# Local attention in a decoder kernel: heads of a pair on two halves of the array's rows, grouped scores and values, and VectorE in program order

## The chip, the core and the metric

The kernel runs on one core of a Trainium2 chip. A core has five engines that each work through a queue of their own: TensorE (PE in the profile; its weight loads have a row of their own, PEld), VectorE (DVE), ScalarE (ACT), GpSimd (POOL) and SyncE (SP), which here issues nearly all DMAs. TensorE writes its results to PSUM, a small memory of eight banks of 512 floats on each of 128 partitions; VectorE and ScalarE take them from there to SBUF. The metric is the device time of one execution in microseconds.

## The reference, cut to what matters

Three stages follow one another on 8 sequences of 256 tokens with 128 features. A state-space block and a cross-attention come first; the change touches the third stage, a stack of six layers:

```
for i in range(DEPTH):                     # 6
    x = attn_layer(shift_tokens(x), ...) + x
    x = ffn_layer(shift_tokens(x), ...) + x

def attn_layer(x, Wqkv, qs, ksc, Wo):      # 16 heads of 64 features
    q, k, v = jnp.split(x @ Wqkv, 3, -1)
    q, k = l2norm(q) * qs, l2norm(k) * ksc
    q, k = rotary(q), rotary(k)
    return local_attention(q, k, v) @ Wo

def local_attention(q, k, v):              # windows of 32 queries
    # each window sees its own 32 keys and the 32 before them
    sim = einsum('bhwie,bhwje->bhwij', bq, bk2) * 8
    attn = softmax(where(mask, -max, sim), -1)
    return einsum('bhwij,bhwje->bhwie', attn, bv2)
```

All of it is in 32-bit floats. For one sequence and layer there are 8 windows and 16 heads, so 128 small products of 32 queries by 64 keys over 64 features, and as many of 32 queries by 64 features over 64 keys.

## The kernel before

The third stage is a software pipeline over `n`, which counts pairs of layer and sequence: 6 x 8 = 48 iterations. `run(n)` (L982) walks through a list `slots` (L949), which is written by hand: four quarters, each with one of the four attention tiles of a sequence. A tile `t` is a half `wh` of the sequence (four windows) and a half `g` of the heads (four pairs of two heads). An entry such as `(scores, 0, 2)` calls that function for iteration `n + 0`.

The steps of one tile, in the order of its data:

- `query_key` (L664): two products of 128x512 on TensorE (L656) give queries or keys of 128 tokens; VectorE multiplies them by two tables out of PSUM (L673, L674), GpSimd adds the two parts of the rotation (L677, two instructions), ScalarE squares (L679).
- `squares` (L686), `root` and `normalise` (L705, GpSimd) divide by the norm; `turn` (L712) transposes eight blocks on TensorE, and ScalarE copies them to `qT` (L719) or to the keys `kz` (L725).
- `scores`: 16 products (L760). The rows of the array hold the 128 features of a pair of heads, and the keys `kz` of the two heads stand in two columns blocks with zeros in the other head's rows, so that one product of 128 rows and 128 columns gives both heads' scores. Four windows' heads use four strips of 32 columns of the array at once (`tile_position=(0, i * W)`). VectorE adds the mask (L768) and takes the maximum (L773), GpSimd subtracts it (L774).
- `weigh`: ScalarE's exponential (L94). `add_weights`: VectorE's sum (L786) and reciprocal (L787), and GpSimd's multiplication by it (L788).
- `turn_weights`: four transposes on TensorE (L795) and ScalarE's copy (L799).
- `attend`: again 16 products of 128 rows and 128 columns (L807), with the values `vz` of two heads in blocks among zeros, which `place` has spread by DMA (L745); VectorE transposes the result in blocks of 32 (L817).
- `project_out`: eight products (L826) and VectorE's addition to the stream (L831).

A feed-forward generator runs once for two sequences and is advanced by the entries `("ff",)` and `("late",)`: nine steps over two iterations, with its products at L872, L877, L893 and L921.

A 32-bit product is two pairs of instructions on TensorE, each a weight load and a matmul, so the counts of L760 and L807 in the profile are twice the number of products. Transposes are one pair each.

The order of instructions on an engine: TensorE's is that of the program (`tc.manual_schedule(engines={PE})`, L1134), so the list `slots` is its queue. The other engines' queues are ordered by a planner at build time, which simulates the program and gives an engine, among the instructions that are ready, the one that the program has first. On the chip each queue is then worked through as it stands. In PSUM, tiles come from a pool with three tags: `big` (two of two banks), `s` (two of one bank) and `o` (two of one bank), eight banks in all.

Of the kernel before, what the change touches and what calls it, by code (L numbers as in the profile page):

```python
# [9 lines left out]
FP = mybir.dt.float32  # L10
# [39 lines left out]
def decoder_kernel(ctx: ExitStack, tc: tile.TileContext, a: dict, out: bass.AP):  # L50
# [656 lines left out]
    def turn(n, c, tb):  # L707

        t = got[n][c, tb]
        t_ps = ps_big("qkT_ps")  # L710
        for hb in range(NHB):
            T.transpose(  # L712
                t_ps[:, hb * P : (hb + 1) * P],
                t[:, 2 * hb : 2 * hb + 2, :].rearrange("p h d -> p (h d)"), ident,
            )
# [12 lines left out]
    def spread(v, wh, g):  # L728


        vz = fixed3["vzs"].pop(0)
        fixed3["vzs"].append(vz)
        for j in range(4):
            w = 4 * wh + j
            for e in range(2):

                at = max(0, (w - 1) * W)
                end = (w + 1) * W
                while at < end:
# [5 lines left out]
                    nc.sync.dma_start(  # L745
                        out=vz[k : k + n, j, :, e, :], in_=src[:, 4 * g : 4 * g + 4, e, :]
                    )
                    at += n
        return vz

    def scores(n, t):


        wh, g = tiles3[t]
        qT, kz = got[n]["qT", wh], fixed3["kzs"][0]
        s_ps = ps_s("s3_ps")
        for j in range(4):
            k0 = (4 * wh + j) * W
            for i in range(4):
                T.matmul(  # L760
                    s_ps[i * W : (i + 1) * W, j * P : (j + 1) * P],
                    lhsT=qT[:, 4 * g + i, j * W : (j + 1) * W],
                    rhs=kz[:, 4 * g + i, :, k0 : k0 + 2 * W], start=True, stop=True,
                    tile_position=(0, i * W),
                )
        shape = [P, 4, 2, 2 * W]
        pw = pools3["b"].tile(shape, FP, name="pw", bufs=4)
        V.tensor_tensor(  # L768
            pw, s_ps.rearrange("p (w e k) -> p w e k", w=4, e=2),
            fixed3["mask"][:, 4 * wh : 4 * wh + 4, :].unsqueeze(2).to_broadcast(shape), ALU.add,  # L770
        )
        mx = pools3["b"].tile([P, 2, 4, 2], FP, name="mx", bufs=4)
        V.tensor_reduce(mx[:, 0], pw, AX.X, ALU.max)  # L773
        G.tensor_tensor(pw, pw, mx[:, 0].unsqueeze(3).to_broadcast(shape), ALU.subtract)  # L774
        got[n]["pw", t] = pw, mx

    def place(n, t):
        got[n]["vz", t] = spread([got[n].get(("v", tb)) for tb in range(2)], *tiles3[t])
# [11 lines left out]
    def turn_weights(n, t):  # L790

        pw, mx = got[n]["pw", t]
        t_ps = ps_o("pT_ps")
        for j in range(4):
            T.transpose(  # L795
                t_ps[:, j * P : (j + 1) * P], pw[:, j].rearrange("p e k -> p (e k)"), ident
            )
        pT = pools3["b"].tile([P, 4, P], FP, name="pT")
        turned.append(A.copy(pT.rearrange("p j q -> p (j q)"), t_ps))  # L799
        got[n]["pT", t] = pT  # L800

    def attend(n, t):
        pT, vz = got[n]["pT", t], got[n]["vz", t]
        o_ps = ps_o("o3_ps")
        for j in range(4):
            for i in range(4):
                T.matmul(  # L807
                    o_ps[i * W : (i + 1) * W, j * P : (j + 1) * P],
                    lhsT=pT[:, j, i * W : (i + 1) * W],
                    rhs=vz[:, j, i].rearrange("p e d -> p (e d)"), start=True, stop=True,  # L810
                    tile_position=(0, i * W),
                )

        wh, g = tiles3[t]
        if g == 0:
            got[n]["oT", wh] = pools3["b"].tile([P, NHB, P], FP, name="oT3")
        V.transpose(  # L817
            got[n]["oT", wh][:, 4 * g : 4 * g + 4, :].rearrange("p k (w q) -> p w k q", w=4),
            o_ps.rearrange("p (w k q) -> p w k q", w=4, k=4),
        )  # L820

    def project_out(n, wh):
        d, b = seq[n]
        y_ps = ps_s("y3_ps")
        for hb in range(NHB):
            T.matmul(  # L826
                y_ps[:, :P], lhsT=wts[d][0][:, hb, :], rhs=got[n]["oT", wh][:, hb, :],
                start=(hb == 0), stop=(hb == NHB - 1),
            )
# [95 lines left out]
    def finish(p, b=None):  # L925
# [22 lines left out]
    q, k = 0, 1  # L948
    slots = [  # L949

        (weigh, 0, 1), (place, 0, 1), (value, 1, 0),
        (attend, -1, 3), (scores, 0, 2), (squares, 1, k, 0), (add_weights, 0, 0),
        ("end", 0), (turn, 1, q, 0), ("end", 1), ("ff",),
        (turn_weights, 0, 0), (root, 1, k, 0), ("late",), (query_key, 1, k, 1),
        (normalise, 1, k, 0),

        ("end", 1), (weigh, 0, 2), (place, 0, 2), (project_out, -1, 1),
        (attend, 0, 0), (scores, 0, 3), (squares, 1, k, 1), (add_weights, 0, 1),
        (turn, 1, k, 0), ("end", 0), ("ff",),
        (turn_weights, 0, 1), (query_key, 2, q, 0), (root, 1, k, 1), (normalise, 1, k, 1),  # L960
        (shift, 3),

        (weigh, 0, 3), (place, 0, 3), (value, 1, 1),
        (attend, 0, 1), (scores, 1, 0), (squares, 2, q, 0), (add_weights, 0, 2),
        (turn, 1, q, 1), ("end", 0), ("end", 1), ("ff",),
        (turn_weights, 0, 2), (query_key, 2, q, 1), (root, 2, q, 0), (normalise, 2, q, 0),

        (weigh, 1, 0), (place, 1, 0), (project_out, 0, 0),
        (attend, 0, 2), (scores, 1, 1), (squares, 2, q, 1), (add_weights, 0, 3),
        (turn, 1, k, 1), ("end", 0), ("end", 1), ("ff",),  # L970
        (turn_weights, 0, 3), (query_key, 2, k, 0), (root, 2, q, 1), (normalise, 2, q, 1),
    ]

# [11 lines left out]
    def run(n):  # L985
        nonlocal ff
        for f, *args in slots:
# [7 lines left out]
                    next(end)  # L995
            elif 0 <= n + k < len(seq) and (f, n + k, *args) not in done:
                f(n + k, *args)
                if f is project_out and k < 0:
# [36 lines left out]
    with tc.tile_pool(name="s2", bufs=2, reuse_waits="tile") as sp:  # L1035
# [26 lines left out]
        def values(v, oT, b, hb, w, ws):  # L1062


            o_ps = ps_o("o2_ps")
            for kb in range(2):
                for e in range(2):
                    c = (2 * hb + e) * HD
# [12 lines left out]
            with_table(A.activation, den, den, AF.Exp, scale=-1.0)  # L1081
            V.tensor_tensor(oT[:, hb, b * S : (b + 1) * S], o_ps[:, :S], den, ALU.mult)

        load_table()
        todo = [(b, hb) for b in range(2) for hb in range(NHB)]
        nxt = first
# [32 lines left out]
    with ExitStack() as st:  # L1119
# [3 lines left out]
        nc.sync.dma_start(out=fixed3["mask"], in_=a["c_mask"])  # L1123


        fixed3["kzs"] = [cp.tile([P, NHB, 2, W + S], FP, name=f"kz{i}") for i in range(1)]
        fixed3["vzs"] = [cp.tile([P, 4, 4, 2, HD], FP, name=f"vz{i}") for i in range(3)]
        for t in fixed3["kzs"] + fixed3["vzs"]:
            G.memset(t, 0.0)
        x3.extend(new_x(p) for p in range(NPAIR))  # L1130

        with tc.manual_schedule(engines={mybir.EngineType.PE}):
            shift(1)
            for n in range(-1, len(seq)):  # L1134
                run(n)
            attend(len(seq) - 1, 3)
            for _ in ff:
                pass
            next(end)
# [96 lines left out]
```

## Time and profile before

| | |
|---|---|
| median of 3 runs | 2316.2 us (2311.98 to 2318.99) |
| the profiled execution | 2310.31 us |
| its span, first to last instruction | 2308.5 us |
| granted TensorE clock, mean | 0.976 |
| busy: PE, DVE, ACT, POOL | 2149.5, 1784.3, 1489.8, 1645.3 us |
| third stage alone | from about 690 us to the end |

A row of the profile names the engine, the line of the kernel, the operation, the tile written and the tiles read, the shape, and a count. In the groups, busy time in us and the mean of one in ns follow; behind a bar stands the engine's idle time just before and whose work ended it. In the timeline the first number is the start in us, the second the time from the first start to the last end of a run of like instructions. The end of a matmul is modelled, with its latency in it: what counts for TensorE is from one start to the next.

### The profile page before, as it was taken

Reading aid. Unit: us, or ns where it says so; the run is one execution under the profiler, and the core shown is the slowest. Engines: PE = TensorE matmul, PEld = TensorE weight load, DVE = VectorE, ACT = ScalarE, POOL = GpSimd, SP = SyncE. Lnnn points to the kernel's source line nnn. Section 1 sums busy time; section 2 is a strip of 40 time slices with the busy share of each in tenths; the row PEclk is TensorE's granted clock in tenths of the full one; section 3 lists DMA queues with packets and bytes.
Section 4 is the critical chain, followed back from the end, with each engine's and each line's share of the span. In section 5 each row is a group of like instructions: output and inputs, shape, how many; then the busy total and the mean of one; then the engine's idle time right before and its main releaser. Section 6 shows DMA issues by size and latency. Waiting matters only on the chain.

```text
span 2308.5 us, 52803 instructions
## 1 busy us (share of the span) xinstructions
PE 2149.5 (93%) x20194; PEld 1337.3 (58%) x20194; DVE 1784.3 (77%) x2558; ACT 1489.8 (65%) x2505; POOL 1645.3 (71%) x1437
## 2 busy tenths in 40 slices
PE   7776888999999999999999999999999999999986
PEld 3232333444446666666666666666666666666664
DVE  5798786354558888888888888888888888888873
ACT  4544554455556776776777676777776777777664
POOL 3889795232478878777787777787877777777760
PEclk7988998999999999999999999999999999999999
DMA  4344341000213334333343334343344334333331
GB/s 121 98 113 99 89 110 33 3 3 1 86 26 56 66 61 89 68 72 59 70 80 71 69 63 88 67 73 63 67 81 72 71 62 77 60 64 62 55 67 32
DMA packets 438228, 153.84 MB, mean 67 GB/s; under 512 B 401886, under 2 KB 418140, under 8 KB 437852
## 3 DMA queue, kind: packets, MB, share of 16 engines
q1 hardware_dynamic: 437500, 150.10, 33.1%
q8 instruction: 162, 2.65, 0.5%
q14 instruction: 86, 0.70, 0.1%
q10 hardware_dynamic: 480, 0.38, 0.1%
HBM read 54.68 MB, written 1.31 MB: 24 GB/s over the span
## 4 chain that ended last, share of the span: by engine, by line
PE 31%; ACT 21%; DVE 20%; POOL 9%; issue 6%; DMA 1%; SPq 0%; POOLq 0%; ACTq 0%; DVEq 0%
DVE rb L674 5%; DVE qk L673 5%; PE qk_ps L656 4%; ACT sq L679 4%; ACT kz L725 3%; POOL pw L774 3%; PE f_ps L893 3%; POOL qk L677 3%; ACT pw L94 3%; DVE ss L686 2%; PE qkT_ps L712 2%; PE o_ps L807 2%; PE y_ps L826 2%; PE s_ps L1050 2%; DVE mx L786 2%
## 5 line engine op out<-in xcount | busy, mean ns | idle before, releaser
L677 POOL TENSOR_TENSOR qk<-qk,rb 128x512 f32<-128x512 f32 x384 | 484.5, 1282 | 108.9 <-DVE rb L674 88.8
L705 POOL TENSOR_TENSOR qk<-qk,rn 128x1024 f32<-128x1024 f32 x192 | 366.3, 1908 | 134.5 <-ACT rn L94 107.5
L656 PE MATMUL qk_ps<-wqkv,xs 128*128 128x512 f32 x768 | 364.4, 597 | 2.0 <-ACT sq L679 2.0
L679 ACT ACTIVATE sq<-qk_ps 128x1024 f32<-128x1024 f32 x192 | 196.7, 1025 | 178.1 <-DVE rb L674 174.7
L673 DVE TENSOR_TENSOR qk<-qk_ps,tab 128x1024 f32<-128x1024 f32 x192 | 233.2, 1215 | 80.8 <-PE qk_ps L656 79.9
L774 POOL TENSOR_TENSOR pw<-pw,mx 128x512 f32<-128x512 f32 x192 | 200.2, 1043 | 91.6 <-DVE mx L773 86.2
L686 DVE TENSOR_REDUCE ss<-sq 128x16 f32<-128x1024 f32 x192 | 232.4, 1211 | 39.5 <-ACT sq L679 36.8
L674 DVE TENSOR_TENSOR rb<-qk_ps,tab 128x1024 f32<-128x1024 f32 x192 | 233.0, 1213 | 0.0
L712 PE MATMUL qkT_ps<-ident,qk 128*128 128x128 f32 x1536 | 209.5, 279 | 15.0 <-ACT v L699 9.8
L94 ACT ACTIVATE pw<-pw 128x512 f32<-128x512 f32 x192 | 120.5, 628 | 154.9 <-POOL pw L774 154.7
L725 ACT COPY kz<-qkT_ps 64x1024 f32<-64x1024 f32 x192 | 193.2, 1006 | 35.3 <-PE qkT_ps L712 33.6
L807 PE MATMUL o_ps<-vz,pT 128*32 128x128 f32 x6144 | 207.5, 276 | 8.2 <-ACT pT L799 8.2
L788 POOL TENSOR_TENSOR pw<-pw,mx 128x512 f32<-128x512 f32 x192 | 200.3, 1044 | 19.0 <-DVE mx L787 17.3
L826 PEld LDWEIGHTS y_ps<-oT,wo 128*128 128x128 f32 x1536 | 186.3, 192 | 44.7 <-issue 37.3
L786 DVE TENSOR_REDUCE mx<-pw 128x8 f32<-128x512 f32 x192 | 130.4, 679 | 105.4 <-ACT pw L94 104.8
L807 PEld LDWEIGHTS o_ps<-vz,pT 128*32 128x32 f32 x6144 | 156.0, 109 | 91.8 <-ACT rn L94 35.6
L1059 POOL TENSOR_TENSOR ws<-w 128x512 f32<-128x512 f32 x64 | 81.4, 1272 | 175.6 <-ACT w L94 162.8
L760 PE MATMUL s_ps<-kz,qT 128*32 128x128 f32 x6144 | 203.0, 273 | 0.0
L656 PE MATMUL v_ps<-wqkv,xs 128*128 128x512 f32 x384 | 186.5, 608 | 16.6 <-ACT kz L725 16.6
L712 PEld LDWEIGHTS qkT_ps<-ident,qk 128*128 128x128 f32 x1536 | 165.2, 141 | 55.2 <-issue 43.6
L500 POOL TENSOR_TENSOR mc<-m,rows 128x512 f32<-128x512 f32 x128 | 164.5, 1288 | 40.5 <-PE d_ps L413 18.7
L826 PE MATMUL y_ps<-oT,wo 128*128 128x128 f32 x1536 | 187.2, 275 | 0.1
(187 smaller groups left out, 4163.6 us busy)
## 6 DMA issues: line engine op xcount, KB each, us to landing
vz<-v SPq DMA_DIRECT2D x1152, 64.0 KB, 2.2
rows<-bc_dram SPq DMA_DIRECT2D x126, 256.0 KB, 3.9
vz<-v SPq DMA_DIRECT2D x576, 32.0 KB, 2.3
wqkv<-in_L_ffn_Wqkv SPq DMA_DIRECT2D x18, 512.0 KB, 4.0
wo<-in_L_ffn_Wo SPq DMA_DIRECT2D x48, 64.0 KB, 2.2
w<-in_L_ffn_W SPq DMA_DIRECT2D x6, 341.0 KB, 3.5
t_in<-in_x SPq DMA_DIRECT2D x4, 256.0 KB, 4.7
wkv<-in_L_xattn_Wkv SPq DMA_DIRECT2D x1, 1024.0 KB, 7.8
```

What stands on the lines that cost most here:

```text
L656: T.matmul(pr[:, i * 512 : (i + 1) * 512], lhsT=got[n]["xs"][:, tb * P : (tb + 1) * P], rhs=thirds[seq[n][0], c][:, i * 512 : (i + 1) * 51 ...
L673: V.tensor_tensor(t, p3, cs, ALU.mult)
L674: V.tensor_tensor(rb, p3, sn, ALU.mult)
L677: G.tensor_tensor(t[:, :, o], t[:, :, o], rb[:, :, f], ALU.add)
L679: A.activation(sq, p3, AF.Square)
L686: V.tensor_reduce(got[n]["ss"][:, 2 * c + tb, :], got[n]["sq"], AX.X, ALU.add)
L705: G.tensor_tensor(t, t, r, ALU.mult)
L712: T.transpose(t_ps[:, hb * P : (hb + 1) * P], t[:, 2 * hb : 2 * hb + 2, :].rearrange("p h d -> p (h d)"), ident,)
L725: A.copy(fixed3["kzs"][0][r, :, e, W + tb * P : W + (tb + 1) * P], t3[r])
L774: G.tensor_tensor(pw, pw, mx[:, 0].unsqueeze(3).to_broadcast(shape), ALU.subtract)
L807: T.matmul(o_ps[i * W : (i + 1) * W, j * P : (j + 1) * P], lhsT=pT[:, j, i * W : (i + 1) * W], rhs=vz[:, j, i].rearrange("p e d -> p (e d) ...
L826: T.matmul(y_ps[:, :P], lhsT=wts[d][0][:, hb, :], rhs=got[n]["oT", wh][:, hb, :], start=(hb == 0), stop=(hb == NHB - 1),)
```

## The change

It has these parts, all for the third stage unless said:

- `kz` has no zeros any more: `[P, NHB, W + S]` in place of `[P, NHB, 2, W + S]`, and `turn` writes it in one copy of 128 partitions in place of two of 64.
- `scores` works for a half `wh` of the sequence, thus two tiles in one group. Each product has 64 rows (one head) and 64 columns; the two heads `e` of a pair stand on the halves of the array's rows (`tile_position=(e * HD, i * W)`). There are 64 products in place of 2 x 16. They write to a new PSUM tile of two banks, `ps_two` (one buffer), a bank for each head.
- `masked` (mask and allocation) and `peak` (maximum, and GpSimd's subtraction) are what `scores` did behind its products.
- `attend` likewise: 64 products of 64 rows and 64 columns for two tiles in one group, in the same PSUM tile, and two transposes on VectorE. `vz` is half as large, in six buffers in place of three. `oT` has another layout, which `project_out` reads in four runs of 32.
- `turn_weights` takes its PSUM from tag `s`; the tag `o` is gone here. In the second stage `values` takes the two banks of one `ps_two` in turn.
- `slots` is written anew: scores in the first and third quarter, `attend` in the second and fourth, `project_out` later than before. `add_weights` and `turn_weights` of a tile stay in one quarter, in front of that quarter's `query_key`.
- VectorE's order is that of the program, as TensorE's is.
- The feed-forward's addition of `ff_b` (L880) goes from VectorE to ScalarE.

```
+    def ps_two(name):
+        return banks[-1].tile([P, 2, 512], FP, tag="two", name=name, bufs=1)
...
-            for e in range(2):
-                r = slice(e * HD, (e + 1) * HD)
-                copied.append(
-                    A.copy(fixed3["kzs"][0][r, :, e, W + tb * P : W + (tb + 1) * P], t3[r])
-                )
+            copied.append(A.copy(fixed3["kz"][:, :, W + tb * P : W + (tb + 1) * P], t3))
...
-    def scores(n, t):
...
-            for i in range(4):
-                T.matmul(
-                    s_ps[i * W : (i + 1) * W, j * P : (j + 1) * P],
-                    lhsT=qT[:, 4 * g + i, j * W : (j + 1) * W],
-                    rhs=kz[:, 4 * g + i, :, k0 : k0 + 2 * W], start=True, stop=True,
-                    tile_position=(0, i * W),
-                )
+    def scores(n, wh):
+        qT, kz = got[n]["qT", wh], fixed3["kz"]
+        s_ps = ps_two("s3_ps")
+        for g in range(2):
+            for j in range(4):
+                k0 = (4 * wh + j) * W
+                for i in range(4):
+                    for e in range(2):
+                        r = slice(e * HD, (e + 1) * HD)
+                        c = (4 * g + j) * 2 * W
+                        T.matmul(
+                            s_ps[i * W : (i + 1) * W, e, c : c + 2 * W],
+                            lhsT=qT[r, 4 * g + i, j * W : (j + 1) * W],
+                            rhs=kz[r, 4 * g + i, k0 : k0 + 2 * W], start=True, stop=True,
+                            tile_position=(e * HD, i * W),
+                        )
+        got[n]["s_ps"] = s_ps
...
+    def attend(n, wh):
+        o_ps = ps_two("o3_ps")
+        for g in range(2):
+            pT, vz = got[n]["pT", 2 * wh + g], got[n]["vz", 2 * wh + g]
+            for j in range(4):
+                for i in range(4):
+                    for e in range(2):
+                        r = slice(e * HD, (e + 1) * HD)
+                        c = (4 * g + j) * HD
+                        T.matmul(
+                            o_ps[i * W : (i + 1) * W, e, c : c + HD],
+                            lhsT=pT[r, j, i * W : (i + 1) * W], rhs=vz[r, j, i, :],
+                            start=True, stop=True, tile_position=(e * HD, i * W),
+                        )
+        oT = got[n]["oT", wh] = pools3["b"].tile([P, 2, 2, 4 * HD], FP, name="oT3")
+        for g in range(2):
+            V.transpose(oT[:, g], o_ps[:, :, g * 256 : (g + 1) * 256])
...
-        V.tensor_scalar(xn, xn, col("ff_b", d), None, ALU.add)
+        A.activation(xn, xn, AF.Identity, bias=col("ff_b", d))
...
+        (weigh, 0, 1), (place, 0, 1), (value, 1, 0), (scores, 0, 1), (add_weights, 0, 0),
+        ("end", 0), (masked, 0, 2), (masked, 0, 3), (squares, 1, k, 0), (turn, 1, q, 0),
+        (peak, 0, 2), ("end", 1), ("ff",),
+        (turn_weights, 0, 0), (query_key, 1, k, 1), (root, 1, k, 0), (normalise, 1, k, 0),
+
+        ("end", 1), (weigh, 0, 2), (place, 0, 2), (project_out, -1, 0), (add_weights, 0, 1),
+        (attend, -1, 1), (squares, 1, k, 1), (turn, 1, k, 0),
+        (peak, 0, 3), ("end", 0), ("ff",),
+        (turn_weights, 0, 1), (query_key, 2, q, 0), (root, 1, k, 1), (normalise, 1, k, 1),
+        (shift, 3),
...
-        with tc.manual_schedule(engines={mybir.EngineType.PE}):
+        with tc.manual_schedule(engines={mybir.EngineType.PE, mybir.EngineType.DVE}):
```

The third and fourth quarter are the first and second over again, with other indices; `("late",)` stands in the third in place of the first.

More of the change, by code (lines that the diff above doesn't have):

```diff
@@ L745, in spread @@
                     nc.sync.dma_start(
-                        out=vz[k : k + n, j, :, e, :], in_=src[:, 4 * g : 4 * g + 4, e, :]
+                        out=vz[k : k + n, j, :, :], in_=src[:, 4 * g : 4 * g + 4, e, :]
                     )
@@ L749, in spread, with masked, peak @@
         return vz
-    def scores(n, t):
-        wh, g = tiles3[t]
[L755 to L758, printed above, removed]
-            for i in range(4):
-                T.matmul(
-                    s_ps[i * W : (i + 1) * W, j * P : (j + 1) * P],
-                    lhsT=qT[:, 4 * g + i, j * W : (j + 1) * W],
-                    rhs=kz[:, 4 * g + i, :, k0 : k0 + 2 * W], start=True, stop=True,
-                    tile_position=(0, i * W),
-                )
+    def scores(n, wh):
[15 more added lines that the diff above has]
+        got[n]["s_ps"] = s_ps
+    def masked(n, t):
+        wh, g = tiles3[t]
         shape = [P, 4, 2, 2 * W]
-        pw = pools3["b"].tile(shape, FP, name="pw", bufs=4)
+        pw = pools3["b"].tile(shape, FP, name="pw", bufs=5)
         V.tensor_tensor(
-            pw, s_ps.rearrange("p (w e k) -> p w e k", w=4, e=2),
+            pw,
+            got[n]["s_ps"][:, :, g * 256 : (g + 1) * 256].rearrange("p e (w k) -> p w e k", w=4),
             fixed3["mask"][:, 4 * wh : 4 * wh + 4, :].unsqueeze(2).to_broadcast(shape), ALU.add,
         )
-        mx = pools3["b"].tile([P, 2, 4, 2], FP, name="mx", bufs=4)
+        got[n]["pw", t] = pw, pools3["b"].tile([P, 2, 4, 2], FP, name="mx", bufs=5)
+    def peak(n, t):
+        pw, mx = got[n]["pw", t]
         V.tensor_reduce(mx[:, 0], pw, AX.X, ALU.max)
-        G.tensor_tensor(pw, pw, mx[:, 0].unsqueeze(3).to_broadcast(shape), ALU.subtract)
-        got[n]["pw", t] = pw, mx
+        G.tensor_tensor(pw, pw, mx[:, 0].unsqueeze(3).to_broadcast([P, 4, 2, 2 * W]), ALU.subtract)
     def place(n, t):
@@ L792, in turn_weights @@
         pw, mx = got[n]["pw", t]
-        t_ps = ps_o("pT_ps")
+        t_ps = ps_s("pT_ps")
         for j in range(4):
@@ L797, in turn_weights @@
             )
-        pT = pools3["b"].tile([P, 4, P], FP, name="pT")
+        pT = pools3["b"].tile([P, 4, P], FP, name="pT", bufs=4)
         turned.append(A.copy(pT.rearrange("p j q -> p (j q)"), t_ps))
         got[n]["pT", t] = pT
[L802 to L820, printed above, removed]
+    def attend(n, wh):
[15 more added lines that the diff above has]
+            V.transpose(oT[:, g], o_ps[:, :, g * 256 : (g + 1) * 256])
     def project_out(n, wh):
@@ L826, in project_out @@
             T.matmul(
-                y_ps[:, :P], lhsT=wts[d][0][:, hb, :], rhs=got[n]["oT", wh][:, hb, :],
+                y_ps[:, :P], lhsT=wts[d][0][:, hb, :],
+                rhs=got[n]["oT", wh][:, hb // 4, (hb // 2) % 2, :].rearrange(
+                    "p (w h q) -> p h w q", w=4, h=2
+                )[:, hb % 2],
                 start=(hb == 0), stop=(hb == NHB - 1),
@@ L949, in decoder_kernel @@
     slots = [
[L951 to L959, printed above, removed]
+        (weigh, 0, 1), (place, 0, 1), (value, 1, 0), (scores, 0, 1), (add_weights, 0, 0),
[5 more added lines that the diff above has]
+        (peak, 0, 3), ("end", 0), ("ff",),
         (turn_weights, 0, 1), (query_key, 2, q, 0), (root, 1, k, 1), (normalise, 1, k, 1),
         (shift, 3),
[L963 to L970, printed above, removed]
+        (weigh, 0, 3), (place, 0, 3), (value, 1, 1), (scores, 1, 0), (add_weights, 0, 2),
+        ("end", 0), (masked, 1, 0), (masked, 1, 1), (squares, 2, q, 0), (turn, 1, q, 1),
+        (peak, 1, 0), ("end", 1), ("ff",),
+        (turn_weights, 0, 2), (root, 2, q, 0), ("late",), (query_key, 2, q, 1),
+        (normalise, 2, q, 0),
+        (weigh, 1, 0), (place, 1, 0), (project_out, -1, 1), (add_weights, 0, 3),
+        (attend, 0, 0), (squares, 2, q, 1), (turn, 1, k, 1),
+        (peak, 1, 1), ("end", 0), ("end", 1), ("ff",),
         (turn_weights, 0, 3), (query_key, 2, k, 0), (root, 2, q, 1), (normalise, 2, q, 1),
@@ L997, in run @@
                 f(n + k, *args)
-                if f is project_out and k < 0:
+                if f is project_out and args[0]:
                     d, b = seq[n + k]
@@ L1062, in values @@
         def values(v, oT, b, hb, w, ws):
-            o_ps = ps_o("o2_ps")
+            o_ps = o2_ps[:, hb % 2, :]
             for kb in range(2):
@@ L1082, in values @@
             V.tensor_tensor(oT[:, hb, b * S : (b + 1) * S], o_ps[:, :S], den, ALU.mult)
+        o2_ps = ps_two("o2_ps")
         load_table()
@@ L1123, in decoder_kernel @@
         nc.sync.dma_start(out=fixed3["mask"], in_=a["c_mask"])
-        fixed3["kzs"] = [cp.tile([P, NHB, 2, W + S], FP, name=f"kz{i}") for i in range(1)]
-        fixed3["vzs"] = [cp.tile([P, 4, 4, 2, HD], FP, name=f"vz{i}") for i in range(3)]
-        for t in fixed3["kzs"] + fixed3["vzs"]:
+        fixed3["kz"] = cp.tile([P, NHB, W + S], FP, name="kz")
+        fixed3["vzs"] = [cp.tile([P, 4, 4, HD], FP, name=f"vz{i}") for i in range(6)]
+        for t in [fixed3["kz"]] + fixed3["vzs"]:
             G.memset(t, 0.0)
         x3.extend(new_x(p) for p in range(NPAIR))
-        with tc.manual_schedule(engines={mybir.EngineType.PE}):
+        with tc.manual_schedule(engines={mybir.EngineType.PE, mybir.EngineType.DVE}):
             shift(1)
@@ L1135, in decoder_kernel @@
                 run(n)
-            attend(len(seq) - 1, 3)
+            project_out(len(seq) - 1, 0)
+            attend(len(seq) - 1, 1)
             for _ in ff:
```

## The prediction

> **What bounds the kernel now.** I read the shares by engine first (PE 93%, DVE 77%, POOL 71%), then the timeline of TensorE in the steady part of the third stage, because a share alone doesn't say whether an engine is waited for. One quarter of an iteration:
>
> ```profile
> 1407.09 1.08 PE L807 MATMUL o_ps<-vz,pT 128*32 128x128 f32 x32
> 1407.98 1.06 PE L760 MATMUL s_ps<-kz,qT 128*32 128x128 f32 x32
> 1408.97 1.09 PE L712 MATMUL qkT_ps<-ident,qk 128*128 128x128 f32 x8
> 1409.90 1.46 PE L921 MATMUL f_ps<-fh,w 128*128 128x256 f32 x6
> 1411.20 0.60 PE L795 MATMUL pT_ps<-ident,pw 128*128 128x128 f32 x4
> 1411.64 1.88 PE L656 MATMUL qk_ps<-wqkv,xs 128*128 128x512 f32 x4
> 1413.36 1.88 PE L656 MATMUL v_ps<-wqkv,xs 128*128 128x512 f32 x4
> 1415.17 1.08 PE L807 MATMUL o_ps<-vz,pT 128*32 128x128 f32 x32
> ```
>
> No row waits: TensorE goes from one piece to the next, so its work sets the pace. From start to start: values 0.89, scores 0.99, transposes 0.93, feed-forward 1.30, weights' transposes 0.44, queries 1.72, values' projection 1.81. The quarters repeat every two iterations (eight quarters; start to start of L795: 8.28, 7.71, 9.94, 7.71, 8.75, 8.15, 8.08, 7.50), 66.1 us or 8.27 a quarter, 24 times over.
>
> The one stall of L795 on the weights' multiplication is at the start of the stage, and it shows a path that the steady part keeps slack on. I took these rows from the timeline of all engines:
>
> ```profile
> 702.66 2.74 PE L656 MATMUL qk_ps<-wqkv,xs 128*128 128x512 f32 x4
> ...
> 705.44 1.22 DVE L673 TENSOR_TENSOR qk<-qk_ps,tab 128x1024 f32<-128x1024 f32 x1 [1.91 <-PE qk_ps L656]
> ...
> 706.59 1.21 DVE L674 TENSOR_TENSOR rb<-qk_ps,tab 128x1024 f32<-128x1024 f32 x1
> ...
> 707.72 0.19 DVE L787 RECIPROCAL mx<-mx 128x8 f32<-128x8 f32 x1
> ...
> 708.14 2.51 POOL L677 TENSOR_TENSOR qk<-qk,rb 128x512 f32<-128x512 f32 x2
> ...
> 710.61 2.05 POOL L788 TENSOR_TENSOR pw<-pw,mx 128x512 f32<-128x512 f32 x2
> ...
> 711.71 0.66 PE L795 MATMUL pT_ps<-ident,pw 128*128 128x128 f32 x4 [1.68 <-POOL pw L788]
> ```
>
> The reader is to see that the reciprocal is done at 707.9, but GpSimd's multiplication L788 stands behind the two sums of the rotation (L677) and starts at 710.61, and that L795 waits for it. From the modelled end of the queries (702.66 + 2.74 = 705.40) to L795 it took 6.31. In the steady part L788 ends 3.4 to 11 us ahead of its L795, because the planner has moved the sum L786 and its reciprocal ahead of L673 on VectorE.
>
> **The change, part by part.** *Row halves.* The trace has no matmul of 64 rows by 32 columns. Nearest are these groups:
>
> ```profile
> L807 PE MATMUL o_ps<-vz,pT 128*32 128x128 f32 x6144 | 207.5, 276 | 8.2 <-ACT pT L799 8.2
> ...
> L1050 PE MATMUL s_ps<-qT,kT 64*128 64x256 f32 x512 | 73.8, 402 | 3.3 <-ACT sq L679 2.9 <-DVE w L1056 0.3
> ```
>
> L807 keeps four column strips going: 32 matmuls in eight turns of 0.109 us, in each of which the four start 0.007 apart. L1050 (row halves, two banks) takes 1.07 for eight matmuls of 256 columns, where one after another would need about 8 x 0.215 = 1.72, so halves of the rows do run at once. With eight tiles and 64 columns a turn is about 0.056, and a group of 128 matmuls has 16 turns: 0.90 at best. Against that, issue: the records of TensorE's semaphore instructions, 16 instructions apart, stand 0.125 apart with 0.051 for themselves, so about 4.6 ns an instruction, and 256 instructions take 1.2. The Trainium skill speaks against the change here: "TensorE: Matmul & The Clock Gate", section "Wait — 56ns, not 53.3ns?", says that matmuls never start less than about 25 ns apart however few columns they have. By that rule a group costs 128 x 0.025 = 3.2. The average of L807, 0.109 / 4 = 27 ns, does not refute it; starts 7 ns apart on different strips do, for short runs. I take 1.1, nearer to the trace, and keep 0.9 and 3.2. A quarter has one such group in place of L807 and L760, with one entry and one exit of the tiled mode as before: 1.88 becomes about 1.2, **0.7 less in 192 quarters, 134 us of TensorE's time**. By the page's rule it would be 1.4 more, 270 us.
>
> *Key copies:* 192 of 1006 ns become 96 of about 1012 (the row of the queries' copy): 96 us less on ScalarE, which waits and isn't the bound; nothing, hidden under TensorE. *The bias* L880 leaves VectorE (1831 ns, 24 times) for ScalarE (about 650, by L94 on the same shape): nothing on the path. *DMAs:* the same nine a tile with the same runs; SyncE issues each in about 0.65, 5.9 of 8.3 a quarter, still enough. Six buffers end its waits for L807, of which no reader waits. *One PSUM tile* for scores and values: a quarter lies between a group and the next, and VectorE reads it within about 2 us of its end; nothing unless VectorE is over 4 us late. *The memset* of kz halves, from 3.9: at most 2 us once. *Second stage:* the same two banks in turn; nothing.
>
> *VectorE in program order* is what decides. In `slots`, `add_weights` stands behind the `query_key` of the quarter before, so L786 and L787 now come behind L673 and L674. GpSimd's two sums are ready when L674 ends, the multiplication only 0.9 later, and the sums are first in the program too; the planner will queue sums, multiplication. `turn_weights` of the same tile and then `query_key` stand at the end of that same quarter on TensorE. This closes a loop, once a quarter: queries from start to modelled end 1.88; VectorE starts 0.04 behind; L673 and L674 2.35 (the median in the trace); 0.08; two sums 2.50; L788 1.04; 0.05; L795 0.44, and the next queries. **Sum 8.38.** The one occurrence above gives 6.31 + 0.49 + 1.88 = 8.68. I take 8.45. All waiting of other engines hangs on this loop: behind L795 on TensorE stand the queries, and so VectorE's and ScalarE's next work; what TensorE saves becomes its wait for L788 (own work up to L795: 1.81 + 1.2 + 0.93 and on average 1.2 of feed-forward, 5.1, while the loop lets L795 go at 6.1).
>
> Only the quarter with the three upward products (6 x 0.43 = 2.58) is longer by TensorE: 1.81 + 1.2 + 0.93 + 2.58 + 0.44 + 1.72 = 8.7. Eight quarters: 7 x 8.45 + 8.7 = 67.9, against 66.1: +1.8, 24 times, **+43**. The first six quarters, where TensorE has little to do (6.9 to 7.6 now), become 8.45: +8. GpSimd's table work at five layer borders (eight instructions, 3.3 us, of which 1.5 shows now) falls into the loop: up to +1.8 each, I take +5. Memset -2. Together +54 on the profiled 2310; the median stands 6 above that execution, so the forecast is 2316 + 54 = **2370 us**.
>
> **Rivals.** *GpSimd multiplies before the sums, or between them.* The loop loses 1.25 to 2.5, TensorE bounds again, and 0.7 x 8 = 5.6 is gained 24 times: 2316 - 134 = 2182 us. It decides as soon as the loop falls under 8.27, only 0.2 less than I take. For it: the order is a planner's, which I can't see. Against it: at the start of the stage, and at 1400.75, where a reciprocal had been issued at 1400.31, the sums went first; nothing stands between the two sums anywhere in the trace. *Issue bounds the groups* by the page's 25 ns: TensorE reaches L795 2 us later, the loop no longer matters, 9.6 a quarter: 2316 + 250 = about 2570. It decides from about 17 ns a matmul. *The loop is slack but VectorE's order is not:* its work of 6.9 a quarter plus waits at the head of its queue bounds at about 8: 2265 us. *Nothing happens:* the halves don't run at once; then a group costs 1.8 as before, and the loop still rules: the main case.
>
> **How the numbers follow.** Loop bound 0.68 (its own range 2322 to 2425: loop 8.3 to 8.7); multiplication first 0.20 (2150 to 2240); VectorE 0.04; issue 0.08. A measurement of this kernel tells 0.3%, 7 us, from no change. Slower: 0.63 of the main case and 0.08; same 0.03; faster 0.20 + 0.04 + 0.02 of the main case. Leaving out the lower part of the second case and the issue case, the range is 2180 to 2430.
>
> **What would show it.** Right: L795 waits for POOL L788 in nearly every quarter, about 1 us; TensorE's busy time falls by some 130 us while the span grows; POOL's queue reads sums, multiplication; L807 and L760 take 0.9 to 1.3 a group. Wrong: TensorE without gaps and a quarter of 7.6, or groups over 2 us.

## The result, and the profile after

The changed kernel takes 2406.5 us (median of 4, 2402.7 to 2411.4), the kernel before beside it 2314.1 (2310.4 to 2319.0): a ratio of 1.040, 95% interval 1.038 to 1.041. It is slower by 92 us; I had forecast 54. The page of the kernel after: its engine totals, its instruction queue (packets, MB), its chain by line, and two of its groups (busy us, mean ns of one | idle just before, and what ended it):

```profile
PE 2131.7 (89%) x32482; PEld 1297.4 (54%) x32482; DVE 1742.5 (73%) x2533; ACT 1423.0 (59%) x2438; POOL 1645.6 (69%) x1440
...
q8 instruction: 255, 4.18, 0.8%
...
POOL qk L681 17%; PE qk_ps L660 13%; POOL pw L799 7%; DVE qk L677 7%; DVE rb L678 6%; PE pT_ps L806 5%; PE f_ps L907 2%; PE y_ps L837 2%; PE o_ps L1083 2%; PE pr L241 2%; PE v_ps L660 2%; PE s_ps L1064 2%; PE s_ps L764 2%; PE y_ps L1121 1%; PE o_ps L823 1%
...
L677 DVE TENSOR_TENSOR qk<-qk_ps,tab 128x1024 f32<-128x1024 f32 x192 | 234.9, 1224 | 297.3 <-PE qk_ps L660 297.3
...
L806 PE MATMUL pT_ps<-ident,pw 128*128 128x128 f32 x768 | 127.6, 289 | 137.3 <-POOL pw L799 134.3
```

The line numbers have moved: the queries are L660 (before L656), their two multiplications L677 and L678 (L673, L674), the sums of the rotation L681 (L677), the sum and reciprocal of the weights L797 and L798 (L786, L787), GpSimd's multiplication L799 (L788), the transposes of the weights L806 (L795), scores L764 (L760), values L823 (L807).

The first six entries of the chain are one circle: queries, two multiplications, rotation, multiplication of the weights, transposes. TensorE's transposes L806 stood 134 us behind L799, in 145 of the 192 quarters (0.9 us each), where L795 had hardly stood at all. One turn of the circle, from the timeline of the kernel after:

```profile
1402.30 0.66 PE L806 MATMUL pT_ps<-ident,pw 128*128 128x128 f32 x4
...
1402.79 1.88 PE L660 MATMUL qk_ps<-wqkv,xs 128*128 128x512 f32 x4
...
1404.71 1.23 DVE L677 TENSOR_TENSOR qk<-qk_ps,tab 128x1024 f32<-128x1024 f32 x1 [0.73 <-PE qk_ps L660]
1405.85 1.22 DVE L678 TENSOR_TENSOR rb<-qk_ps,tab 128x1024 f32<-128x1024 f32 x1
1406.39 1.77 PE L823 MATMUL o_ps<-vz,pT 64*32 64x64 f32 x128
...
1407.21 2.51 POOL L681 TENSOR_TENSOR qk<-qk,rb 128x512 f32<-128x512 f32 x2 [1.56 <-PE o_ps L823]
1407.89 0.20 DVE L798 RECIPROCAL mx<-mx 128x8 f32<-128x8 f32 x1
1408.09 1.09 PE L716 MATMUL qkT_ps<-ident,qk 128*128 128x128 f32 x8
...
1409.68 1.04 POOL L799 TENSOR_TENSOR pw<-pw,mx 128x512 f32<-128x512 f32 x1
...
1410.77 0.66 PE L806 MATMUL pT_ps<-ident,pw 128*128 128x128 f32 x4 [0.30 <-POOL pw L799]
```

The reciprocal is done at 1408.09, but GpSimd is in its sums until 1409.7, and only then multiplies. From one L806 (1402.30) to the next (1410.77) is 8.47. (A releaser such as "PE o_ps L823" on L681 is only the last event that the profile saw; the sums needed L678, which ended then.) The group of values takes 1.70 here from its start to the start of the next piece, not 1.2.

Where the 92 us lie can be read from the first and the last of the weights' transposes, in the views of these lines of before and after (shortest, median and longest of a matmul in ns; first and last start):

```profile
L795 PE MATMUL pT_ps<-ident,pw x768: 270/273/421, 693.5 to 2269.3; 128*128 128x128 f32 x192
```

```profile
L806 PE MATMUL pT_ps<-ident,pw x768: 271/273/474, 707.5 to 2346.1; 128*128 128x128 f32 x192
```

| part of the span, us | before | after | more | forecast |
|---|---|---|---|---|
| to the first weights' transposes | 693.5 | 707.5 | +14.0 | -2 |
| from there to the last | 1575.8 | 1638.6 | +62.8 | +56 |
| from the last to the end | 39.2 | 54.8 | +15.6 | 0 |
| span | 2308.5 | 2400.9 | +92.4 | +54 |

So the loop, on which the forecast rested, has about the size it was given. What was missing is mostly in two stretches outside the steady part, 16 us each.

### The profile page after: what moved, and what is told of

Same layout as the page of the kernel before. It is cut to its first block, busy times and chain, and to the rows that moved or that the text cites. A ratio compares the mean times of both kernels' runs of the same rounds, so it can differ in the third digit from the quotient of the medians.

```text
span 2400.9 us, 76914 instructions
## 1 busy us (share of the span) xinstructions
PE 2131.7 (89%) x32482; PEld 1297.4 (54%) x32482; DVE 1742.5 (73%) x2533; ACT 1423.0 (59%) x2438; POOL 1645.6 (69%) x1440
## 3 DMA queue, kind: packets, MB, share of 16 engines
q8 instruction: 255, 4.18, 0.8%
## 4 chain that ended last, share of the span: by engine, by line
PE 39%; POOL 26%; DVE 16%; issue 3%; ACT 3%; DMA 1%; SPq 0%; POOLq 0%; ACTq 0%; DVEq 0%
POOL qk L681 17%; PE qk_ps L660 13%; POOL pw L799 7%; DVE qk L677 7%; DVE rb L678 6%; PE pT_ps L806 5%; PE f_ps L907 2%; PE y_ps L837 2%; PE o_ps L1083 2%; PE pr L241 2%; PE v_ps L660 2%; PE s_ps L1064 2%; PE s_ps L764 2%; PE y_ps L1121 1%; PE o_ps L823 1%
## 5 line engine op out<-in xcount | busy, mean ns | idle before, releaser
L681 POOL TENSOR_TENSOR qk<-qk,rb 128x512 f32<-128x512 f32 x384 | 481.7, 1277 | 182.6 <-DVE rb L678 137.6
L677 DVE TENSOR_TENSOR qk<-qk_ps,tab 128x1024 f32<-128x1024 f32 x192 | 234.9, 1224 | 297.3 <-PE qk_ps L660 297.3
L660 PE MATMUL qk_ps<-wqkv,xs 128*128 128x512 f32 x768 | 369.4, 604 | 2.2 <-ACT kz L726 1.1
L786 POOL TENSOR_TENSOR pw<-pw,mx 128x512 f32<-128x512 f32 x192 | 202.3, 1054 | 91.0 <-DVE mx L785 90.8
L806 PE MATMUL pT_ps<-ident,pw 128*128 128x128 f32 x768 | 127.6, 289 | 137.3 <-POOL pw L799 134.3
L678 DVE TENSOR_TENSOR rb<-qk_ps,tab 128x1024 f32<-128x1024 f32 x192 | 233.2, 1214 | 0.0
L806 PEld LDWEIGHTS pT_ps<-ident,pw 128*128 128x128 f32 x768 | 81.7, 142 | 251.6 <-POOL pw L799 248.5
L799 POOL TENSOR_TENSOR pw<-pw,mx 128x512 f32<-128x512 f32 x192 | 200.8, 1046 | 15.8 <-DVE mx L798 12.7
L810 ACT COPY pT<-pT_ps 128x512 f32<-128x512 f32 x192 | 112.5, 586 | 146.1 <-PE pT_ps L806 143.2
L660 PEld LDWEIGHTS qk_ps<-wqkv,xs 128*128 128x128 f32 x768 | 133.5, 194 | 98.8 <-issue 95.2
L482 PE MATMUL y<-mc,ident 128*128 128x512 f32 x256 | 148.9, 699 | 42.0 <-POOL mc L504 41.8
L660 PE MATMUL v_ps<-wqkv,xs 128*128 128x512 f32 x384 | 180.6, 592 | 0.3 <-ACT sq L683 0.3
L502 DVE TENSOR_TENSOR_SCAN m<-dw,ab 128x256 f32<-128x256 f32 x256 | 159.9, 668 | 26.1 <-POOL mc L504 21.8
L764 PEld LDWEIGHTS s_ps<-kz,qT 64*32 64x32 f32 x12288 | 137.6, 105 | 74.4 <-DVE qk L677 69.0
```

The source lines that it names most:

```text
L660: T.matmul(pr[:, i * 512 : (i + 1) * 512], lhsT=got[n]["xs"][:, tb * P : (tb + 1) * P], rhs=thirds[seq[n][0], c][:, i * 512 : (i + 1) * 51 ...
L677: V.tensor_tensor(t, p3, cs, ALU.mult)
L678: V.tensor_tensor(rb, p3, sn, ALU.mult)
L681: G.tensor_tensor(t[:, :, o], t[:, :, o], rb[:, :, f], ALU.add)
L786: G.tensor_tensor(pw, pw, mx[:, 0].unsqueeze(3).to_broadcast([P, 4, 2, 2 * W]), ALU.subtract)
L799: G.tensor_tensor(pw, pw, mx[:, 1].unsqueeze(3).to_broadcast([P, 4, 2, 2 * W]), ALU.mult)
```

## The experiments

The theory: the order of VectorE and GpSimd closes the loop, and TensorE waits in it. Rivals: TensorE itself is the bound, because 128 small matmuls cost it too much; or VectorE's program order as such is harmful, whatever stands in it.

**e1: the sum of the weights ahead of the queries.** One entry of `slots` is moved in each quarter, from behind the previous quarter's `query_key` to ahead of it:

```diff
-  (scores, 0, 1), (add_weights, 0, 0),
+  (scores, 0, 1),
 ...
-  (turn_weights, 0, 0), (query_key, 1, k, 1), (root, 1, k, 0), ...
+  (turn_weights, 0, 0), (add_weights, 0, 1), (query_key, 1, k, 1), (root, 1, k, 0), ...
```

and so in the other three quarters.

> Changed kernel with one thing moved: add_weights of the next quarter stands ahead of query_key in each quarter, so VectorE sums a tile's weights before it touches the queries, and GpSimd multiplies (L799) before it adds the rotation (L681). Loop theory: the wait of the weights' transposes L806 for L799 (137 us) goes, TensorE sets the pace again with what the smaller groups leave of its work, 66.1 - 8 x 0.25 = 64.1 us in eight quarters against 68.5 now; 24 x 4.4 = 106 us less, and the slow first quarters with them: 2280 to 2305 us. TensorE theory (the groups of 128 small matmuls cost so much that TensorE is the bound by itself): 2395 to 2415. Theory that VectorE's program order as such bounds, whatever stands in it: 2380 to 2415, with the wait of L806 moved to another line.

Measured: 2255.5 us, ratio to before 0.975 (0.974 to 0.977), 151 us less than the changed kernel. The timeline of e1:

```profile
1403.10 0.68 DVE L797 TENSOR_REDUCE mx<-pw 128x8 f32<-128x512 f32 x1
...
1403.81 0.20 DVE L798 RECIPROCAL mx<-mx 128x8 f32<-128x8 f32 x1
...
1404.27 1.23 DVE L677 TENSOR_TENSOR qk<-qk_ps,tab 128x1024 f32<-128x1024 f32 x1 [0.26 <-PE qk_ps L660]
...
1405.73 1.04 POOL L799 TENSOR_TENSOR pw<-pw,mx 128x512 f32<-128x512 f32 x1
...
1406.73 2.50 POOL L681 TENSOR_TENSOR qk<-qk,rb 128x512 f32<-128x512 f32 x2
...
1408.91 0.60 PE L806 MATMUL pT_ps<-ident,pw 128*128 128x128 f32 x4
```

GpSimd now multiplies ahead of the sums, and the product is there 2 us before L806 at 1408.9. L806's waits for L799 in this run come to 2.8 us. Eight quarters (starts of L806: 7.52, 9.90, 7.43, 8.16, 8.01, 7.74, 7.00, 6.84) take 62.6 us against 68.5 after and 66.1 before. I had expected 64.1 from groups of 1.6; about half of the 1.5 us between is waits of TensorE that the kernel before had and this one has not (26.5 us for L656, L712 and L893 between 780 and 2100 us there, 13.5 for L907 here). So both rivals fall: the same groups of matmuls on TensorE, and VectorE in program order as well, are faster than the kernel before.

**e2: VectorE in program order alone**, in the kernel before.

```diff
-  with tc.manual_schedule(engines={mybir.EngineType.PE}):
+  with tc.manual_schedule(engines={mybir.EngineType.PE, mybir.EngineType.DVE}):
```

> Kernel before with one thing of the change: VectorE also in program order; its slots, its groups of 32 matmuls over 128 rows and its planner for GpSimd stay. In these slots the sum of the weights stands behind the mask and maximum of the scores of the same quarter, so the loop is longer than in the changed kernel: queries 1.7, values' projection 1.8 (every second quarter), values 0.9, scores 1.0, mask and maximum 1.2, squares 1.1, sum and reciprocal 0.7, multiplication 1.04, transposes 0.44, so 8.2 to 10.1 a quarter, 9.3 on average against 8.27. Loop theory: 2316 + 192 x 1.0 = about 2510 (2420 to 2620). TensorE theory (order is harmless, the groups cost): 2310 to 2325.

Measured: 2969.4 us, ratio 1.286 (1.279 to 1.292). The direction is the loop's, the size was far off (2420 to 2620 expected). L795 waits in nearly every quarter, from TensorE's waits in e2:

```profile
PE pT_ps L795 <- POOL pw L788: 461.8, 190, 4.5
```

A quarter takes 10.6 where the clock is full, since in these slots mask, maximum and squares all stand between the scores and the sum of the weights on VectorE. My sum had 9.3: it left out the output projection (L826, 1.9 us), which stands in the loop in every quarter that has no values' projection. More than half of the quarters take 11.5 us or more. There TensorE's clock is low: the queries take 2.7 to 3.6 us in each of them (3.47 at 1498.54) and 1.88 in the others, and the run's mean clock is 0.898. The kernel before lives from the planner's order of VectorE.

**e3: row halves, groups and slots alone**, the change with VectorE given back to the planner (the line of e2 reversed).

> Changed kernel with VectorE given back to the planner: row halves, two tiles in one group and the new slots stay. Loop theory: the planner takes the sum of the weights as soon as it is ready, GpSimd multiplies early, L806 hardly waits, TensorE bounds at about 8.0 a quarter: 2275 to 2305. TensorE theory: 2395 to 2415. The second stage keeps its later end (stage three's first weights' transposes near 707 us instead of 693) by either.

Measured: 2336.7 us, ratio 1.010 (1.008 to 1.011). Better than the changed kernel by 70, worse than before by 23, and not the 2275 to 2305 that the loop theory said. The loop is open (4.1 us for L799 in all), but the planner's order gives TensorE other waits, here those of the whole run:

```profile
PE f_ps L907 <- ACT sq L683: 18.2, 43, 0.6
PE pT_ps L806 <- DVE x L845: 17.9, 22, 0.9
...
PE y_ps L837 <- DVE ln_xc L887: 10.7, 21, 0.6
PE y_ps L837 <- DVE x L936: 10.7, 22, 0.6
```

With two smaller ones they come to 61 us between 780 and 2100, or 3 in eight quarters: 66.6 against e1's 62.6. So row halves, groups and new slots together bring nothing under the planner's order, and e1, with program order on VectorE and the sum in its place, is 81 us faster than e3. What each part is worth alone is not shown: no run has the row halves in the old slots. In the three parts of the span, e3 has +18.1, -9.3 and +16.7 against before.

**e4: two PSUM tiles in the second stage.** In the change the values of the second stage are halves of one tile that lives through the whole stage; here they are two tiles taken in turn, in a pool of their own that is closed before the third stage takes the banks.

```diff
-  o_ps = o2_ps[:, hb % 2, :]
+  o_ps = twos[-1].tile([P, 512], FP, tag="o", name="o2_ps")
```

> Changed kernel with the second stage's values in two PSUM tiles of one bank each that are taken in turn, as before the change, instead of two halves of one tile; the third stage's double tile is opened behind it in the same banks. If the halves of one tile are held apart only as a whole (TensorE waits 51 times, 37.8 us, for the division L1096 of the pair just before), these waits go and everything of the third stage starts 12 to 15 us earlier: 2390 to 2396. If the later start of the third stage came from elsewhere (memsets, loads, the planner's order): 2403 to 2410.

Measured: 2389.9 us, 16.6 less than the changed kernel; the first weights' transposes start at 693.9, as before the change (693.5). What had delayed them is in the view of the line L1083 of the kernel after, the idle time ahead of it (us, times; weight loads and matmuls together):

```profile
its engine sat idle before it (us, times) until:
  DVE oT L1096: 37.8, 51
```

The first product of most pairs waited for the division of the pair just before, though that reads the other bank. The program's waits are set by whole tiles, so a writer of one half also waits for the reader of the other. With two tiles these waits are 4.1 us, five times.

**e5 and e9: work put into TensorE's waits at the start.** The first quarters of the third stage last 10.1 us in the changed kernel (starts of L806 from 707.5: 10.1, 10.1, 10.1, 10.2, 10.1, then 8.5). TensorE's timeline there:

```profile
717.57 1.09 PE L806 MATMUL pT_ps<-ident,pw 128*128 128x128 f32 x4 [4.33 <-POOL pw L799]
718.46 3.17 PE L660 MATMUL qk_ps<-wqkv,xs 128*128 128x512 f32 x4
721.47 1.88 PE L660 MATMUL v_ps<-wqkv,xs 128*128 128x512 f32 x4
...
727.72 1.02 PE L806 MATMUL pT_ps<-ident,pw 128*128 128x128 f32 x4 [1.94 <-POOL pw L799]
728.54 3.25 PE L660 MATMUL qk_ps<-wqkv,xs 128*128 128x512 f32 x4
```

and its clock, from the table by stretches of the same kernel (the granted clock is the third number from the right):

```profile
730.00:740.00 10.00, 6.62 (x145) 4.04 (x144) 6.02 (x8) 3.96 (x10) 6.42 (x5) 0.84 0.24 41
...
760.00:770.00 10.00, 8.16 (x161) 5.38 (x160) 7.16 (x9) 6.28 (x12) 7.61 (x7) 1.00 0.38 66
```

The same queries take 1.88 or 3.2: just behind the wait they run at about half speed, and they lie in the loop. The Trainium skill, "TensorE: Matmul & The Clock Gate", Part 1, tells of such a gate that halves the clock after about 3.4 us without work. In this trace gaps of 1.8 and 1.9 us were followed by slow queries too. The test adds products that nobody reads ahead of L806:

```diff
+  w_ps = ps_s("warm_ps")
+  for _ in range(3 if n else 6):       # e5, n < 2; e9: 2, in the first six quarters
+      T.matmul(w_ps, lhsT=ident, rhs=thirds[0, 0][:, :512], start=True, stop=True)
```

> Changed kernel with work added: ahead of the weights' transposes L806 of the first two iterations stand 6 (first) or 3 (second) matmuls 128x128 by 512 columns whose result nobody reads, 36 in all or 15.5 us at 0.43 each, in time in which TensorE waited 1.6 to 4.3 us. Clock theory (the first five quarters take 10.1 us instead of 8.5 because TensorE, having waited, runs the transposes and the queries at half speed, 1.1 instead of 0.66 and 3.1 to 3.5 instead of 1.88): with the matmuls the queries stay at 1.88 and the first five quarters at 8.4 to 8.8; 6 to 9 us less, 2396 to 2401. If the long quarters come from loads or from the planner's order: 2406 to 2420.

Measured for e5: 2410.9 us, ratio 1.042 (1.040 to 1.044). I had counted a product as one matmul; it is two, so the added work filled more than the waits, and the time came out where the rival (loads, the planner's order) had put it. The rows speak for the clock all the same: it was 1.00 throughout, and the queries took 1.88 in every one of these quarters.

> As e5, with less added work: 2 matmuls of 512 columns ahead of L806 in each of the first six quarters only. In e5 one such matmul showed as two rows of 0.43, so e5 added 46 us of TensorE's time (5.3 or 2.7 a quarter), about all that the clock gave back. Here it is 1.77 us a quarter in waits of 1.6 to 4.3. Clock theory: the queries stay near 1.88 in most of these quarters, the first five take 8.5 to 9.0 instead of 10.1, 5 to 8 us less than the changed kernel's 2406.5: 2398 to 2402. If so little work does not hold the clock, or the clock is not what makes these quarters long: 2406 to 2412.

Measured for e9: 2403.0 us, ratio 1.038 (1.037 to 1.040), which overlaps with the change's, and lies between the two ranges expected. The rows are clearer than the time: six quarters of 8.39 to 8.51, and as soon as the added work ends, the slow quarter comes (10.1).

```profile
723.90 0.66 PE L810 MATMUL pT_ps<-ident,pw 128*128 128x128 f32 x4
724.39 1.88 PE L660 MATMUL qk_ps<-wqkv,xs 128*128 128x512 f32 x4
...
757.71 0.75 PE L810 MATMUL pT_ps<-ident,pw 128*128 128x128 f32 x4 [1.94 <-POOL pw L799]
758.25 3.53 PE L660 MATMUL qk_ps<-wqkv,xs 128*128 128x512 f32 x4
```

So the clock is why the first quarters were 10.1 and not 8.45: the first six take 50.7 us here and 59.1 in the changed kernel. Not all of these 8.4 us stay in the sum, since one slow quarter comes later; from the first transposes to the last it is 1634.3 against 1638.6. Where the limit lies is not settled: in e9 gaps of 2.0 and 2.1 us left the clock at 1.00, and one of 1.94 was followed by queries of 3.53.

**e6: what a group of small matmuls costs.** Three more passes over the scores of eight iterations, with 32 columns (L788), with one row half only (L791), and with the halves in the outer loop (L794):

```diff
+  again([(g, j, i, e) for g in R2 for j in R4 for i in R4 for e in R2], 32, half)
+  again([(g, j, i, 0) for g in R2 for j in R4 for i in R4], 64, one_row_half)
+  again([(g, j, i, e) for g in R2 for j in R4 for e in R2 for i in R4], 64, e_outer)
```

> Changed kernel with three more passes over the scores' group in 8 of its 48 iterations, one behind the other ahead of the mask: 128 matmuls with 32 columns instead of 64 (into half of the columns, so those hold the same scores), then the 64 of one row half alone with 64 columns, then 128 with 64 columns and the row half as the outer loop of each turn. If instructions cost a fixed time each (1.55 us for 128 is 12 ns each), the passes take about 1.55, 0.78 and 1.55. If columns set the time (64 columns and eight tiles at once, plus a fixed part), 32 columns take 0.9 to 1.0, the single half 0.9 to 1.5. If the alternation of row halves costs, the third pass is under 1.3. The time of the whole is longer by 8 x 2 x about 3 us and tells nothing more.

The timeline of TensorE in e6:

```profile
1131.11 1.52 PE L764 MATMUL s_ps<-kz,qT 64*32 64x64 f32 x124
1132.40 0.21 PE L788 MATMUL s_ps<-kz,qT 64*32 64x32 f32 x1
...
1132.47 1.62 PE L788 MATMUL s_ps<-kz,qT 64*32 64x32 f32 x116
1135.88 0.23 PE L788 MATMUL s_ps<-kz,qT 64*32 64x32 f32 x4 [1.78 <-issue]
...
1135.97 1.01 PE L791 MATMUL s_ps<-kz,qT 64*32 64x64 f32 x58
1136.76 0.24 PE L794 MATMUL s_ps<-kz,qT 64*32 64x64 f32 x1
...
1136.82 0.77 PE L794 MATMUL s_ps<-kz,qT 64*32 64x64 f32 x54
1139.62 1.32 PE L794 MATMUL s_ps<-kz,qT 64*32 64x64 f32 x71 [2.04 <-issue]
```

64 columns: 1.29 us for 124 matmuls, 10.4 ns each. 32 columns: 1.62 less the last one's own 0.2, for 116, 12.2 ns each. One row half, thus four tiles: 0.79 for 58, 13.6 ns each. The halves in the outer loop: 0.77 less 0.2 for 54, 10.6 ns each ahead of the pause, so their alternation is not what costs. With eight tiles half the columns don't save time, and what is left is a cost of each matmul with its weight load: 10 to 12 ns, so by estimate 5 to 6 an instruction. So it went as the first of the three cases, except for the single row half. That should have taken 0.78 us and takes 0.87 (64 x 13.6), near the lower end of what I gave for columns (0.9 to 1.5): its four tiles start within 0.056 us, which is the turn of 64 columns that the prediction has. So with four tiles columns can still set the time.

The starts of the single records add one thing. In the changed kernel the first 32 matmuls of every group, in all 192, start 8.3 ns apart, close to the 7 of eight tiles in a turn of 0.056. The other 96 start 11.6 (scores) and 12.6 ns (values) apart in the median. A short run keeps the pace that I took for the whole group; a long one does not. Why it slows down is not shown. The pauses of 1.8 and 2.0 us were not expected either; see the end.

**e7 and e8: the multiplication done twice**, in the changed kernel (e7) and in e1 (e8), to see whether the loop has the length that the sum gives it.

```diff
+  twice = pools3["b"].tile([P, 4, 2, 2 * W], FP, name="twice", bufs=1)
+  G.tensor_tensor(twice, pw, mx[:, 1].unsqueeze(3).to_broadcast([P, 4, 2, 2 * W]), ALU.mult)
   G.tensor_tensor(pw, pw, mx[:, 1].unsqueeze(3).to_broadcast([P, 4, 2, 2 * W]), ALU.mult)
```

> Changed kernel with the multiplication L799 of the weights done twice on GpSimd (first into a scratch tile), 192 instructions of 1.04 us more on an engine that is busy 69%. Loop theory: each lies in the loop; seven quarters of 8.46 become 9.50 and the one of 9.30 becomes 9.5: 76.0 instead of 68.5 in eight, 24 x 7.5 = 180 us more and 5 at the start: 2570 to 2610. Theory that TensorE or VectorE's order bounds and GpSimd has slack: 2405 to 2430.

> The same doubled multiplication in the kernel of e1, where the sum of the weights stands ahead of the queries on VectorE. Loop theory: there the product is done a whole quarter ahead of its reader, GpSimd's work of 6.5 + 1.04 = 7.5 us a quarter is still under TensorE's 62.6 / 8 = 7.8: 2255 to 2290. If GpSimd's multiplication sets the time wherever it stands: 2255 + 180 = about 2435.

Measured: e7 2664.4 us, ratio 1.151 (1.149 to 1.153), 258 more than the changed kernel; e8 2290.7, ratio 0.990 (0.989 to 0.992), 35 more than e1. The same 192 instructions, 200 us of GpSimd, cost more than their length in the loop and a sixth of it outside. In e7 the steady quarter is 9.59 against 8.47, a step of 1.12 for one instruction of 1.04; the quarter with the three upward products went from 9.30 to 10.35, not to 9.5 as I had it; and 33 of the 191 quarters took 10.9 to 12, twelve at the start and the others scattered. In each of these the queries take 2.8 to 3.6 us, in all others 1.88. So behind the longer waits the low clock comes into the steady part too (the run's mean is 0.950 against 0.971), which is why e7 is above what I expected.

**e10 and e11: what the findings give together.** e10 has the edits of e1 and e4; e11 has ScalarE in program order too, behind the last iteration.

> The edits of e1 and e4 together: sum of the weights ahead of the queries, and two PSUM tiles for the second stage's values. The two act in different stages, so their gains add: 2255.5 - (2406.5 - 2389.9) = about 2239 (2235 to 2245). If the third stage's start is held by its loads as well, only a part: 2245 to 2255.

> e10, and behind the last iteration ScalarE is issued in program order too, so the three Gelu of one feed-forward stand together: 5 loads of activation tables fewer (1.28 us each) on ScalarE in the last 40 us, in which TensorE waited up to 5 us for it. If ScalarE's tables make the end longer (from the last weights' transposes to the end 56 us against 39.5 before the change): 6 to 12 us less than e10, about 2230. If the end is longer only because more work is left behind the last transposes: within 3 us of e10.

Measured: e10 2235.6 us, ratio 0.967 (0.965 to 0.968); e11 2231.3, ratio 0.965 (0.963 to 0.966). The two edits of e10 add, as expected. e10 beats both kernels, by 79 and 171 us. e11 cannot be told from e10 by the time. Behind the last weights' transposes e10 loads eight activation tables, e11 four (1.28 us each), but the time from there to the end only fell from 55.0 to 52.1. So tables are the smaller part of the longer end. TensorE's own rows there show the two parts: from the last transposes to the end it works 33.7 us in the changed kernel and 23.3 in the one before, and waits 18.0 and 12.9. In e11 the work is still 33.9 and the waits are 15.0. The longest wait there, before and after, is for the normed input of the upward products. In the changed kernel two instructions of the norm's root (L98) and the addition of `ff_b` (L894) stand among five loads of tables on ScalarE; in e11 this wait is gone.

```profile
2282.84 1.56 PE L893 MATMUL f_ps<-fxn,w 128*128 128x256 f32 x6 [1.75 <-DVE fxn L880]
```

```profile
2372.30 2.93 PE L907 MATMUL f_ps<-fxn,w 128*128 128x256 f32 x6 [5.03 <-ACT fxn L894]
```

## Why the prediction was right or wrong

- **The loop, right.** L806 waits for L799, GpSimd's queue reads sums, multiplication, and the loop has 8.41 to 8.49 against the 8.45 taken. e1 removes it by one entry's place, e7 lengthens it by about what one more instruction takes (1.12 for 1.04).
- **"8.7" for the quarter with the upward products, mis-sized:** 9.30. Eight quarters are 68.5, not 67.9. The term held a group at 1.2; in the quarter from 1444.62 to 1453.92 us it takes 1.62, which is 0.42 of the 0.6. The rest is in the upward products (2.73 for 2.58) and the transposes.
- **"A group of 128 matmuls: 1.1", mis-sized:** 1.52 (scores) and 1.61 (values) in the median, from a group's start to the next piece's. I had 4.6 ns an instruction, from records of semaphores; e6 shows 5 to 6, and the fast pace lasts for 32 of the 128 matmuls. With it goes "134 us of TensorE's time": its busy time fell by 18, and by 59 in e1. For the changed kernel's time it mattered little, as the loop hid it; for the rival "GpSimd multiplies first" it is most of the reason why e1, which does just that, gives 2255 and not 2182; start and end are 29 of these 73 us. The page's 25 ns a matmul, which I set against it, does not hold for tiles of the array that differ: 8 to 14 ns.
- **"Second stage: the same two banks in turn; nothing", failed:** +14. The banks are the same, but what waits is decided by the tile, and there was now one. e4 shows it.
- **"First six quarters: +8", mis-sized:** the first six take 59.1 against 46.7, +12.4. Two errors met here. The six quarters of the kernel before are not all "6.9 to 7.6": the first two took 8.3 and 9.9, so the loop alone makes +4 (6 x 8.45 = 50.7). And the clock was not thought of: the waits that the loop brings slow down the very products in it, which is the other 8.4 (e9 has 50.7).
- **The end of the kernel was not in the sum, failed:** +15.6. It is there in e1 and e3 as well (+16.7), so it comes neither from the loop nor from VectorE's order. By TensorE's rows 10.4 of it is work that the new slots leave behind the last transposes: a second output projection, and 2.0 us of upward and 3.1 of downward products ahead of the last one. The other 5.1 is waits, and e11 takes 3 of it away. "The bias: nothing on the path" holds but for this end, where the addition on ScalarE comes some 1.3 us later than it did on VectorE.
- **Layer borders +5 and the steady +43:** the stretch behind the first six quarters has +50.4 for +48, in part by luck. By the medians the steady part is 2.4 longer in eight quarters (68.5 against 66.1) and not 1.8, some 55 us over the 185 quarters. Against that, four layer borders cost no more than before (about 1.0 over the median, 1.5 before), and the last eleven quarters are shorter by 5.
- **Signs:** L806's wait and GpSimd's order came as named. TensorE's busy time fell by 18, not by some 130, and the groups take more than 1.3.

The range held the time, and so did the main case's own, 2322 to 2425. The direction was earned: the loop came as summed. That 2406 still lies in the range is luck in part: start, first quarters and end, 36 of the 38 us that were missing, were not what the range stood for (a loop of 8.3 to 8.7), and they all made the kernel slower.

## What to carry to other kernels

When an engine's order becomes that of the program, follow one result around all engines until it comes back to its start, and sum one turn of that loop: here an entry that stood one call too late cost 151 us, and moved it made the change a gain. A saving on the busiest engine counts only when no such loop is longer than that engine's work, and a wait that such a loop brings can lower TensorE's clock and so lengthen itself. When two buffers are joined into one tile, look whether readers and writers of its halves are still held apart.

## What the runs showed of the hardware

TensorE's small matmuls on eight different tiles of its array start 8.3 ns apart for the first 32 of a group of 128 in the changed kernel, and 11 to 13 ns behind. In e6, right behind such a group, it was 12 ns with 32 columns as well.

In dense runs of them TensorE pauses for 1.0 to 2.5 us with nothing that it waits for by the profile. In all sixteen dense runs of e6 (448 matmuls each) the first pause comes behind 233 to 276 matmuls and the second exactly 128 later. The changed kernel has 24,111 more instructions than the one before and moves 4.18 MB of them for 2.65, thus about 64 bytes each by estimate. A packet of the instruction queue (16 KB: 4.18 MB in 255) then holds some 256, which are 128 matmuls with their weight loads. That the pauses are code that arrives too late is argued from this, not tested. With other work between the groups of 128 the changed kernel shows no such pause; e1 and e3 show one each (1.7 and 2.0 us).
